# Transposing probabilities on VectorE and through DRAM instead of on TensorE, with scores three units ahead

## The chip, the cores and the metric

The kernel runs on one core of a Trainium2 chip. The core has five engines that run their own instruction streams and meet only at semaphores: TensorE (PE) for matrix products, VectorE (DVE), ScalarE (ACT), GpSimd (POOL), and SyncE (SP), which in this kernel issues every DMA. [...] DMAs move data between DRAM and SBUF. The metric is device time in microseconds of one execution.

## The reference

The input is x, eight blocks (batches) of 128 tokens with 512 features, and a context of the same shape. Four layers follow each other, each added to x after a layernorm: a one-head cross attention, a linear layer with a routed low-rank part, a cross attention with 32 query heads on 8 key/value heads, and a feed-forward layer whose weights are integers.

```python
x = x + xattn0(layernorm(x), ctx, ...)
x = x + W @ layernorm(x) + b + routed low-rank part
x = x + xattn1(layernorm(x), ctx, mask, ...)
x = x + ffn1(layernorm(x), ...)
# xattn1, for each of 32 heads of 128 features, 4 query heads to a key/value head:
q, k = rmsnorm(q) * q_norm_w, rmsnorm(k) * k_norm_w
attn = softmax(q @ k.T / sqrt(128) + mask)        # 128 queries, 128 keys
out  = concat_heads(attn @ v) @ o_proj_w.T
# ffn1: W[g, i] = (int_w - zero[group of 128, i]) * scale[group of 128, i]
y = (silu(h @ gate) * (h @ up)) @ down            # 512 -> 1792 -> 512
```

In the third layer there are eight blocks and eight key/value heads, so 64 pairs of a block and a head. One such pair, with its four query heads, is a *unit*. Every unit projects queries (512 x 512), scores (four 128 x 128 products), takes a softmax, multiplies by the values and projects the outcome (512 x 512) into x.

## The kernel before

[...] Scores are plain fp32 matmuls. A cut is a copy to the rounding format on ACT and a subtraction on DVE (split_fast, lines 64 to 66), or both on POOL (split_pool, lines 60 to 62).

The time has three stages. Up to about 210 us the first two layers run, and the keys and values of all heads are made and written to DRAM (kv_part, kv_out). The attention follows in 64 rounds up to about 710 us. The last stage is the feed-forward layer, in 14 chunks of 128 of the 1792 hidden features. In the first and the last stage a planner orders most of the instructions; in the attention (`tc.manual_schedule()`, line 790) and at the end of the last stage (line 980) every engine runs its instructions in the order in which the program is written, so an instruction that waits holds up all that stand behind it on its engine.

A round is written out in the list ROUND (line 738). Its entries are pairs of an offset and a step: in round n the step works on unit n + offset. The steps of a unit, with the engine of each:

- q_mm (PE): 12 matmuls of the query projection into PSUM. q_ssq (ACT): the sums of squares. q_rms (POOL): the norm factors (lines 346 and 348). q_turn (DVE): the queries times the factors (line 517), then a transpose of each 32x32 square (line 523) into qb. q_write (SP): qb to DRAM. q_read (SP): four DMAs of 64 KB back into qT, arranged so that features lie on partitions and each column holds a query.
- s_mm (PE): four scores products, 8 instructions (line 543). s_max (DVE): adds the mask and takes the maximum. s_exp (ACT): four exponentials with their sums. s_norm: reciprocal on DVE (line 563), scaling on POOL (line 565).
- p_mm (PE): four transposes of the probabilities by a product with the identity into PSUM (line 570). p_cut: the cut of the outcome, ACT (line 574) and DVE (line 575). av_mm (PE): three matmuls with the values. av_cut: the cut, ACT (line 591) and DVE (line 592). o_mm (PE): 12 matmuls of the output projection. o_add (DVE): adds into x (line 604).

The entries in quotation marks are places for background work by round: "load" (weights of coming heads, keys and values from DRAM), "cut" (their cut on POOL), "int" and "sub". The last two prepare the feed-forward weights: int_dma loads a tile of integers and, spread over the partitions by the DMA, its zero points; int_sub subtracts on DVE (line 631) and writes the outcome to DRAM (wint). This is done for 42 tiles, one a round.

Scores run one unit ahead of the output projection, and the query projection four units ahead. The tail has its own list TAIL. While the last rounds run, the feed-forward layer begins: for the first NE = 3 chunks, the gate and up products of the first 512 tokens run as fillers (early_unit, FILL, BANKS), as the layernorm of those tokens (norm_x, norm_turn) is done by then. For these chunks the last stage makes only the second 512 tokens. In the last stage each chunk has four gate units, four up units and four down units (up_unit, down_unit), evicted by ACT (line 875 or 878) or DVE (line 881), sums on POOL (lines 879 and 906), silu on ACT, the product on DVE (line 917), and a cut on ACT (line 921) and POOL (line 928).

Of the kernel before, what the change touches and what calls it, by code (L numbers as in the profile page):

```python
# [34 lines left out]
def f32(ap):  # L35
    return ap.bitcast(F32)
# [3 lines left out]
def tile_layers(ctx: ExitStack, tc: tile.TileContext, t, out: bass.AP):  # L40
# [76 lines left out]
    NE = 3  # L117
# [328 lines left out]
    mask_sb = wk.tile([P, NQ, P], F32, name="mask_sb", bufs=1)  # L446
    ps_q = pool(l1s, "ps_q", 2, PSUM)
# [12 lines left out]
    qps, qss, rqs, qbs, q_d, qTs, sps, nms, sms, prs, tps, pTs, avs, aTs, pos = ({} for _ in range(15))  # L460
# [20 lines left out]
    def k_load(g, hf):  # L481

        kTt[g, hf] = pk.tile([P, NQ, HB, SQ], F32, name="kT")
        for k in range(NQ):
            nc.sync.dma_start(
                kTt[g, hf][k * SQ : (k + 1) * SQ].rearrange("p i b a -> p i (b a)"),
                kT_d[g, hf][:, k, :].rearrange("(i c) e -> c i e", c=SQ),
            )

    def v_load(g, hf):  # L490
        for i, (d, p) in enumerate(((vht, "h"), (vlt, "l"))):
            d[g, hf] = pv.tile([P, HB, HD], F32R, name=f"v{p}")
            nc.sync.dma_start(f32(d[g, hf]).rearrange("p b d -> p (b d)"), v_d[g, hf][i])
# [10 lines left out]
    def q_ssq(u):  # L504
        ssq = qss[u] = small.tile([P, NREP], F32, name="qssq")
        for r in range(NREP):
            junk = wk.tile([P, HD], F32, name="junkq", bufs=2)
# [7 lines left out]
    def q_turn(u):  # L515
# [6 lines left out]
        qb = qbs[u] = wk.tile([P, NQ, NREP, SQ], F32, name="qb")  # L522
# [3 lines left out]

    def q_write(u):
        q_d[u] = dram.tile([P, NQ, NREP * SQ], F32, name=f"q_d{u}")
        nc.sync.dma_start(q_d[u], qbs.pop(u).rearrange("p j r a -> p j (r a)"))

    def q_read(u):

        qTs[u] = wk.tile([P, NQ, NREP * SQ], F32, name="qT", bufs=8)
        for j in range(NQ):
            nc.sync.dma_start(
                qTs[u][j * SQ : (j + 1) * SQ], q_d[u][:, j, :].rearrange("(i c) e -> c i e", c=SQ)
            )
# [29 lines left out]
    def p_mm(u):  # L567
        tp = tps[u] = ps_tr.tile([P, NQ, P], F32, name="tr")
        for r in range(NQ):
            nc.tensor.transpose(tp[:, r, :], prs[u][:, r, :], ident)  # L570

    def p_cut(u):
        ph, pl = pTs[u] = tuple(pat.tile([P, NQ, P], F32R, name=f"pT_{p}") for p in "hl")
        nc.scalar.copy(ph, tps[u])  # L574
        nc.vector.tensor_tensor(pl, tps[u], f32(ph), ALU.subtract)  # L575
# [10 lines left out]
    def av_cut(u):  # L586
        ah, al = aTs[u] = tuple(pat.tile([P, NREP, P], F32R, name=f"aT_{p}") for p in "hl")

        src = avs[u].rearrange("p i (r a) -> p r i a", a=SQ)
        hp, lp = (x.rearrange("p r (i a) -> p r i a", a=SQ) for x in (ah, al))  # L590
        nc.scalar.copy(hp, src)  # L591
        nc.vector.tensor_tensor(lp, src, f32(hp), ALU.subtract)  # L592
# [18 lines left out]
    def int_dma(m, c):  # L611
        wi, zi = (
            wk.tile([P, NREP, P], F32, name="qT", bufs=8).bitcast(I32).rearrange("p r c -> p (r c)")
            for _ in range(2)
        )
        staged[m, c] = (wi, zi)
        if m == "down":
            nc.sync.dma_start(wi, t["down_w"][c * P : (c + 1) * P, :])
            nc.sync.dma_start(zi, t["down_z"][c : c + 1, :].to_broadcast([P, D]))
        else:  # L620
            cols = slice(c * P, (c + 1) * P)
            nc.sync.dma_start(
                wi.rearrange("p (g c) -> p g c", c=P), t[m + "_w"][:, cols].rearrange("(g p) c -> p g c", p=P)
            )
            nc.sync.dma_start(
                zi.rearrange("p (g c) -> p g c", c=P), t[m + "_z"][:, cols].unsqueeze(0).to_broadcast([P, KT, P])
            )

    def int_sub(m, c):
        wi, zi = staged.pop((m, c))  # L630
# [441 lines left out]
```

## Time and profile before

| | |
|---|---|
| time, median of 3 runs | 883.45 us (882.79 to 884.38) |
| the profiled execution's own time | 884.13 us |
| its span in the profile | 882.3 us |
| PE busy | 852.1 us (97%) |
| DVE busy | 626.7 us (71%) |
| POOL busy | 517.5 us (59%) |
| ACT busy | 438.7 us (50%) |
| bytes moved by DMA | 141.07 MB, mean 160 GB/s |
| transposes of the probabilities (line 570) | 256 instructions, 40.1 us busy |
| query writes and reads | 64 of 256 KB and 256 of 64 KB |

The busy time of an engine counts the durations of its instructions. On PE they overlap: a matmul's duration runs from its start to the last result, while the next one has long begun, so starts tell more than durations. A group's line shows the line of the program, engine, operation, the tile written and those read, shapes and count, then busy time and mean duration, and behind the bar the idle time of the engine just before these instructions and what ended it. PEclk is the clock that was granted to TensorE, in tenths of full speed. PEld are the weight loads, which run beside the matmuls.

### The profile page before, as it was taken

To read this page: it belongs to the slowest core of one execution; us is meant where nothing else is said; L and a number is where in the kernel's file an instruction comes from. 1 tells how busy PE (TensorE), PEld (TensorE's weight loads), DVE (VectorE), ACT (ScalarE), POOL (GpSimd) and SP (SyncE) were. 2 spreads that over 40 slices of the span, in tenths; PEclk is the share of its full clock that TensorE was granted. 3 is DMA by queue.
4 is the path that set the end of the run, shared out by engine and by line. 5 is a ranking of instruction groups with operands and counts; after the bars stand their busy time and mean duration, and the time that the engine had idled before them with its cause. 6 is when DMAs were issued, how large, how long until landed. Compare 5 with 4: busy or idle time off the path is not lost.

```text
span 882.3 us, 14414 instructions
## 1 busy us (share of the span) xinstructions
PE 852.1 (97%) x4568; PEld 716.2 (81%) x4568; DVE 626.7 (71%) x1049; ACT 438.7 (50%) x1565; POOL 517.5 (59%) x571
## 2 busy tenths in 40 slices
PE   6999999999999999999999999999999989999976
PEld 5889999899787888888888888888778767788764
DVE  6613797775766677777777677666786887888877
ACT  5324444243544454455544444445555668666652
POOL 4551684234565455555555555775554568899884
PEclk9999999999999999999999999999999999999999
DMA  8522441435787788878788886644344412222103
GB/s 295 138 96 97 143 145 72 134 105 168 237 253 227 221 245 240 218 242 243 229 237 239 243 238 210 187 145 138 110 129 144 132 34 73 72 72 72 48 13 109
DMA packets 141182, 141.07 MB, mean 160 GB/s; under 512 B 17969, under 2 KB 92465, under 8 KB 141105
## 3 DMA queue, kind: packets, MB, share of 16 engines
q1 hardware_dynamic: 141104, 140.14, 53.3%
q8 instruction: 37, 0.61, 0.3%
q14 instruction: 41, 0.33, 0.1%
HBM read 97.62 MB, written 42.47 MB: 159 GB/s over the span
## 4 chain that ended last, share of the span: by engine, by line
PE 79%; DVE 6%; POOL 5%; DMA 5%; issue 2%; ACT 2%; SPq 1%; DVEq 0%; ACTq 0%; POOLq 0%
PE mm L74 8%; PE mm L76 8%; PE mm L75 8%; PE f L870 6%; PE f L871 6%; PE o L76 6%; PE s L543 6%; PE o L75 6%; PE o L74 6%; PE tr L570 3%; PE kv L76 3%; PE kv L75 3%; PE kv L74 3%; DMA qT<-q_d 2%; PE o L584 1%
## 5 line engine op out<-in xcount | busy, mean ns | idle before, releaser
L565 POOL TENSOR_TENSOR pr<-pr,rs 128x512 f32<-128x512 f32 x64 | 66.6, 1040 | 179.6 <-DVE rs L563 176.7
L604 DVE TENSOR_TENSOR xs<-o,xs 128x512 f32<-128x512 f32 x64 | 44.2, 691 | 95.5 <-PE o L76 95.5
L74 PE MATMUL mm<-wq_l,xnT_h 128*128 128x512 f32 x256 | 105.4, 412 | 0.0
L76 PE MATMUL o<-wo_h,aT_l 128*128 128x512 f32 x256 | 100.0, 391 | 0.7 <-DVE aT_l L592 0.7
L74 PE MATMUL o<-wo_l,aT_h 128*128 128x512 f32 x256 | 100.1, 391 | 0.2 <-DVE wo_l L66 0.2
L76 PE MATMUL mm<-wq_h,xnT_l 128*128 128x512 f32 x256 | 100.2, 391 | 0.0
L75 PE MATMUL mm<-wq_h,xnT_h 128*128 128x512 f32 x256 | 100.0, 391 | 0.0
L75 PE MATMUL o<-wo_h,aT_h 128*128 128x512 f32 x256 | 99.7, 390 | 0.0
L574 ACT CAST pT_h<-tr 128x512 fp32r<-128x512 f32 x64 | 37.5, 585 | 121.2 <-PE tr L570 121.2
L557 ACT ACTIVATE pr<-s,nm 128x128 f32<-128x128 f32 x256 | 90.8, 373 | 3.2 <-DVE nm L551 3.0
L591 ACT CAST aT_h<-o 128x512 fp32r<-128x512 f32 x64 | 37.6, 587 | 106.9 <-PE o L584 106.9
L74 PE MATMUL kv<-wkv_l,cT_h 128*128 128x256 f32 x256 | 73.6, 288 | 0.0
L508 ACT ACTIVATE junkq<-mm 128x128 f32<-128x128 f32 x256 | 67.3, 279 | 12.4 <-PE mm L76 6.1
L76 PE MATMUL kv<-wkv_h,cT_l 128*128 128x256 f32 x256 | 73.3, 286 | 0.0
L75 PE MATMUL kv<-wkv_h,cT_h 128*128 128x256 f32 x256 | 72.9, 285 | 0.0
L543 PE MATMUL s<-kT,qT 128*128 128x128 f32 x512 | 68.0, 276 | 1.9 <-DMA qT<-q_d 1.9
L348 POOL TENSOR_TENSOR rrq<-msq,nhalf 128x4 f32<-128x4 f32 x64 | 64.7, 1011 | 5.3
L543 PEld LDWEIGHTS s<-kT,qT 128*128 128x128 f32 x512 | 62.3, 192 | 3.0 <-DMA qT<-q_d 2.8
L575 DVE TENSOR_TENSOR pT_l<-tr,pT_h 128x512 fp32r<-128x512 f32 x64 | 44.0, 688 | 22.8 <-ACT pT_h L574 22.8
L76 PEld LDWEIGHTS o<-wo_h,aT_l 128*128 128x128 f32 x256 | 48.1, 188 | 11.6 <-DVE aT_l L592 1.5
L76 PEld LDWEIGHTS mm<-wq_h,xnT_l 128*128 128x128 f32 x256 | 48.1, 188 | 10.7
L74 PEld LDWEIGHTS o<-wo_l,aT_h 128*128 128x128 f32 x256 | 48.1, 188 | 10.7 <-DVE wo_l L66 0.6
(234 smaller groups left out, 2445.0 us busy)
## 6 DMA issues: line engine op xcount, KB each, us to landing
q_d<-qb SPq DMA_DIRECT2D x64, 256.0 KB, 2.4
qT<-q_d SPq DMA_DIRECT2D x256, 64.0 KB, 3.1
wst<-in_qpT SPq DMA_DIRECT2D x36, 256.0 KB, 3.5
wst<-in_opT SPq DMA_DIRECT2D x36, 256.0 KB, 3.1
wkv<-in_kvT SPq DMA_DIRECT2D x8, 512.0 KB, 4.3
v_d<-vh SPq DMA_DIRECT2D x16, 256.0 KB, 2.1
v_d<-vl SPq DMA_DIRECT2D x16, 256.0 KB, 2.3
kT_d<-kT SPq DMA_DIRECT2D x16, 256.0 KB, 2.6
```

The costliest lines, as they stand in the source:

```text
L74: nc.tensor.matmul(o, ah, bl, start=start, stop=False)
L75: nc.tensor.matmul(o, ah, bh, start=False, stop=False)
L76: nc.tensor.matmul(o, al, bh, start=False, stop=stop)
L348: nc.gpsimd.tensor_tensor(r[:, :n], ms[:, :n], nhalf[:, :n], ALU.pow)
L508: nc.scalar.activation(junk, qps[u][:, r * HD : (r + 1) * HD], AF.Square, accum_out=ssq[:, r : r + 1])
L543: nc.tensor.matmul(sp[:, r, :], qTs[u][:, r, :], kTt[blocks[j]][:, :, i, :], start=True, stop=True)
L557: nc.scalar.activation(pr[:, r, :], sps[u][:, r, :], AF.Exp, bias=nms[u][:, r : r + 1], accum_out=sm[:, r : r + 1])
L565: nc.gpsimd.tensor_tensor(pr, pr, rs.unsqueeze(2).to_broadcast([P, NQ, P]), ALU.mult)
L575: nc.vector.tensor_tensor(pl, tps[u], f32(ph), ALU.subtract)
L604: nc.vector.tensor_tensor(x, pos[u], x, ALU.add)
L870: nc.tensor.matmul(ps[:, hf, :], w, rl, start=True, stop=False)
L871: nc.tensor.matmul(ps[:, hf, :], w, rh, start=False, stop=True)
```

## The change

In the attention:

- p_mm is gone. In its place p_turn transposes each 32x32 square of the probabilities on DVE, p_write writes the outcome to DRAM in one DMA and p_read reads it back in one DMA, so that keys lie on partitions. The cut of the outcome (p_cut) now reads SBUF, and its subtraction runs on POOL.
- q_read is one DMA in place of four. Both reads put the rows on partitions in another order (feature c of square j on partition 4c + j instead of 32j + c), so keys and values are loaded in that order too; the key load is one DMA in place of four.
- Scores run three units ahead of the output projection, the query projection six. The rounds begin at -6, and the last key/value blocks, which stood ahead of the rounds, are put into rounds -6 to -2 ("kv"). TAIL is gone.
- Zero points are loaded once, four DMAs for all tiles (zc). int_sub spreads them over the partitions by a transpose on DVE. Integer weights come from the host in tiles of whole rows; the work is done in three of four rounds.
- Fewer buffers: qT 6 in place of 8, qb and junkq 1 in place of 2.

Around it: five early chunks in place of three, with their fillers behind s_max of the last six rounds; the second layernorm's transposes use another PSUM pool; near the end of the last stage the cast of the product is a step of its own (cast) and stands behind the next silu.

```diff
-    NE = 3
+    NE = 5
...
+        nc.sync.dma_start(
+            kTt[g, hf].rearrange("p i b a -> p i (b a)"), kT_d[g, hf].rearrange("(i c) j e -> (c j) i e", c=SQ)
+        )
...
+    def write(src, name):
+        d = dram.tile([P, NQ, NREP * SQ], F32, name=name)
+        nc.sync.dma_start(d, src.rearrange("p j i a -> p j (i a)"))
+        return d
+
+    def read(dst, d):
+
+        nc.sync.dma_start(dst, d.rearrange("(i c) j e -> (c j) i e", c=SQ))
+
     def q_write(u):
-        q_d[u] = dram.tile([P, NQ, NREP * SQ], F32, name=f"q_d{u}")
-        nc.sync.dma_start(q_d[u], qbs.pop(u).rearrange("p j r a -> p j (r a)"))
+        q_d[u] = write(qbs.pop(u), f"q_d{u}")
 
     def q_read(u):
 
-        qTs[u] = wk.tile([P, NQ, NREP * SQ], F32, name="qT", bufs=8)
-        for j in range(NQ):
-            nc.sync.dma_start(
-                qTs[u][j * SQ : (j + 1) * SQ], q_d[u][:, j, :].rearrange("(i c) e -> c i e", c=SQ)
-            )
+        qTs[u] = wk.tile([P, NQ, NREP * SQ], F32, name="qT", bufs=6)
+        read(qTs[u], q_d[u])
...
-    def p_mm(u):
-        tp = tps[u] = ps_tr.tile([P, NQ, P], F32, name="tr")
-        for r in range(NQ):
-            nc.tensor.transpose(tp[:, r, :], prs[u][:, r, :], ident)
+    def p_turn(u):
+        pb = pbs[u] = wk.tile([P, NQ, NQ, SQ], F32, name="pb", bufs=1)
+        nc.vector.transpose(
+            pb.rearrange("p j i a -> p i j a"), prs.pop(u).rearrange("p i (j c) -> p i j c", c=SQ)
+        )
+
+    def p_write(u):
+        p_d[u] = write(pbs.pop(u), f"p_d{u}")
+
+    def p_read(u):
+
+        tps[u] = wk.tile([P, NREP, P], F32, name="pT")
+        read(tps[u], p_d[u])
 
     def p_cut(u):
-        ph, pl = pTs[u] = tuple(pat.tile([P, NQ, P], F32R, name=f"pT_{p}") for p in "hl")
+        ph, pl = pTs[u] = tuple(pat.tile([P, NREP, P], F32R, name=f"pT_{p}") for p in "hl")
         nc.scalar.copy(ph, tps[u])
-        nc.vector.tensor_tensor(pl, tps[u], f32(ph), ALU.subtract)
+        nc.gpsimd.tensor_tensor(pl, tps[u], f32(ph), ALU.subtract)
...
     def int_sub(m, c):
-        wi, zi = staged.pop((m, c))
-        nc.vector.tensor_tensor(wi.bitcast(F32R), wi, zi, ALU.subtract)
+
+        z = wk.tile([P, NREP, HD], F32, name="q", bufs=1).rearrange("p r d -> p (r d)")
+        nc.vector.transpose(
+            z.rearrange("p (b a) -> p b a", a=SQ),
+            zc[:, MS.index(m), c, :].unsqueeze(2).to_broadcast([P, D // SQ, SQ]),
+        )
+        wi = staged.pop((m, c))
+        nc.vector.tensor_tensor(wi.bitcast(F32R), wi, z, ALU.subtract)
         nc.sync.dma_start(wint[m, c], wi.bitcast(F32))
...
-    FILL = {(NU - 1, p_cut): 3, (NU - 1, s_norm): 2}
-    for n in range(NU - 4, NU - 1):
-        FILL[n, p_cut], FILL[n, s_norm] = 1, 3 if n == NU - 2 else 2
+    FILL = {}
+    for n, m in zip(range(NU - 6, NU), (4, 4, 5, 5, 5, 3)):
+        FILL[n, s_max] = m
...
     ROUND = [
-        (1, s_mm), (3, q_rms), (0, p_cut), (4, q_mm, (0,)), (1, s_max), (0, av_mm), "int", (2, q_read),
-        (0, av_cut), (3, q_turn), (4, q_mm, (1, 2, 3)), (1, s_exp), "load", (3, q_write), "cut", "sub",
-        (0, o_mm), (1, s_norm), (4, q_ssq), (1, p_mm), (0, o_add),
+        "kv", (4, q_read), (5, q_rms), (3, s_mm), (6, q_mm, range(KT)), "cut", (2, p_read), (3, s_max), "int",
+        (3, s_exp), (5, q_turn), (5, q_write), "load", (3, s_norm), (1, av_mm), "sub", (3, p_turn),
+        (3, p_write), (1, av_cut), (6, q_ssq), (2, p_cut), (0, o_mm), (0, o_add),
     ]
...
-        for n in range(NU):
+        kv(-6, NG - 2, 0, 0, 2)
+        at(-6, "load", kv_cut, NG - 1)
+        kv(-5, NG - 2, 1, 0, 2)
+        kv(-4, NG - 1, 0, 0, 2)
+        kv(-3, NG - 1, 1, 0)
+        kv(-2, NG - 1, 1, 2)
+        for n in range(-6, NU):
...
             round_(n)
         norm_turn(NB - 2)
         fillers(3)
         norm_x(NB - 1)
-        fillers(len(fill) - 2)
+        fillers(len(fill) - 4)
         norm_turn(NB - 1)
         fillers(len(fill))
...
         gated(ORDER[-2])
-        rest(ORDER[-2])
         downs("A")
         up_unit("up", 0, c)
         silu(c)
+        cast(ORDER[-2])
+        rest(ORDER[-2])
```

## The prediction

> **What bounds the kernel now.** I read the busy times and the slices first, then the groups of instructions, then one round of the attention on TensorE (PE) as a timeline, then the chain that ended last, and last the waits at the end of the kernel. Busy times and slices of the page:
>
> ```profile
> PE 852.1 (97%) x4568; PEld 716.2 (81%) x4568; DVE 626.7 (71%) x1049; ACT 438.7 (50%) x1565; POOL 517.5 (59%) x571
> ```
>
> ```profile
> PEclk9999999999999999999999999999999999999999
> DMA  8522441435787788878788886644344412222103
> ```
>
> PE is never out of work, at full clock; the others have 29% to 50% to spare; the DMA engines are at 7 to 8 tenths while the attention rounds run. From the groups (busy, mean ns | idle before, and its releaser):
>
> ```profile
> L570 PE MATMUL tr<-ident,pr 128*128 128x128 f32 x256 | 40.1, 279 | 0.7 <-POOL pr L565 0.6
> L604 DVE TENSOR_TENSOR xs<-o,xs 128x512 f32<-128x512 f32 x64 | 44.2, 691 | 95.5 <-PE o L76 95.5
> L565 POOL TENSOR_TENSOR pr<-pr,rs 128x512 f32<-128x512 f32 x64 | 66.6, 1040 | 179.6 <-DVE rs L563 176.7
> ```
>
> VectorE (DVE) spends 95.5 us waiting for PE, GpSimd (POOL) 176.7 us for a row sum; PE waits 0.7 us for its transposes. A busy time is no price on PE, because matmuls overlap; the price is the step from one start to the next. PE in one round (start, duration):
>
> ```profile
> 404.19 0.39 PE L76 MATMUL o<-wo_h,aT_l 128*128 128x512 f32 x1
> 404.42 0.65 PE L570 MATMUL tr<-ident,pr 128*128 128x128 f32 x4
> 404.91 1.06 PE L543 MATMUL s<-kT,qT 128*128 128x128 f32 x8
> 405.72 0.47 PE L74 MATMUL mm<-wq_l,xnT_h 128*128 128x512 f32 x1
> 406.03 0.39 PE L75 MATMUL mm<-wq_h,xnT_h 128*128 128x512 f32 x1
> ```
>
> A 128x512 matmul steps 0.227 us, the four transposes 0.49 (404.91 - 404.42), the scores 0.81, the matmul behind them 0.31. A round of 27 large matmuls is 27 x 0.227 + 0.08 + 0.49 + 0.81 = 7.5 us, and the scores indeed start every 7.5 us from 300 us on. So a round is PE's issue time and nothing else. The chain agrees:
>
> ```profile
> PE 79%; DVE 6%; POOL 5%; DMA 5%; issue 2%; ACT 2%; SPq 1%; DVEq 0%; ACTq 0%; POOLq 0%
> ```
>
> Where PE does wait, from its timeline and the last stage's:
>
> ```profile
> 713.12 0.63 PE L97 MATMUL mm<-ident,xn 128*128 128x128 f32 x4 [1.19 <-DVE xn L91]
> 715.97 0.50 PE L870 MATMUL f<-xnT_l,wf_gate 128*128 128x512 f32 x1 [1.29 <-DVE xnT_l L99]
> ```
>
> ```profile
> 851.68 5.65 POOL L879 TENSOR_TENSOR acc<-acc,tmp 128x1024 f32<-128x1024 f32 x2
> 851.77 3.37 DVE L917 TENSOR_TENSOR th<-th,up 128x1024 f32<-128x1024 f32 x1 [0.43 <-POOL up L906]
> 855.17 1.05 ACT L921 CAST h_h<-th 128x1024 fp32r<-128x1024 f32 x1 [4.64 <-DVE th L917]
> 856.12 1.11 ACT L878 ACTIVATE tmp<-f,sd_sb 128x1024 f32<-128x1024 f32 x1
> 857.28 0.80 PE L870 MATMUL f<-xnT_l,wf_up 128*128 128x512 f32 x1 [4.48 <-ACT tmp L878]
> ```
>
> Two waits for the last layernorm; and one of 4.48 us, where an eviction on ScalarE (ACT) stands behind a cast that waits for a slow product.
>
> **The change, part by part.** The sum runs against the profiled execution: 884.13 us, span 882.3, 1.8 around it. It lies 0.7 above the median of 883.45, taken off at the end. A round is about to be 7.5 - 0.47 = 7.03 us on PE; other work must fit into that.
>
> *Transposes of the probabilities off PE.* 64 x 0.49 = 31.4 us at most. Four layernorm transposes step 0.35 (707.89 to 708.24), and a switch of format might pass to the scores behind them: at least 64 x 0.35 = 22.4. The row of the thing itself is nearer: 0.47, **-30**.
>
> [...]
>
> *What VectorE gets.* Out: the cut of the probabilities (688 ns). In: their turn, p_turn, one stream transpose (713). In 42 rounds, three of four, int_sub turns the zero points first (713) and subtracts (649). Work of a round: 0.69 mask, 0.69 maximum, 0.68 + 0.71 query, 0.16 reciprocal, 0.71, 0.69 aT_l, 0.69 xs = 5.0 us; 6.4 with int_sub. It has to wait for the four exponentials: they run 1.5 us beside 1.4 us of query work (at 407.85 to 409.35 in that round), some 0.35 with the handover. 6.75 < 7.03, so it is hidden by 0.3 us. Without that cover it costs what is over, 42 times.
>
> The subtraction reads two SBUF operands while POOL now scales the probabilities. The trace shows what that can do: the product at 851.77 took 3.37 us with POOL busy, 1.23 at 840.93 with POOL idle. The 42 subtractions of before took 647 to 651 ns each, so none was held up. Bounds: 0 to 0.4 us, the rest of a 1.04 us scaling that began at the reciprocal when the 0.71 us turn ahead is done. At 0.4 a round is 7.15.
>
> [...]
>
> *POOL* gains the cut of the probabilities, now from SBUF, at 1.29 (row of wq_l): 0.19 + 1.01 + 0.62 + 1.29 + 1.04 + 1.29 = 5.44 us. *ACT* keeps 3.8. Both fit.
>
> *The way through DRAM.* p_write and p_read join SP's queue, which loses three of four query reads (0.43 us issue each), three of four key loads and all zero-point loads, so issuing shrinks. But p_read(n+2) waits for a write of the round before; behind it stand the integer load, q_write, the weight loads and p_write, and on POOL the probability cut, the next query's norm factor, the weight cut, the scaling. That closes a loop over two rounds: turn 0.71, write W, read R, cast 0.59, cut 1.29, factor 1.2, weight cut 1.91, scaling 1.04, some 0.3 of handovers = 7.05 + W + R, plus 0.65 for a subtraction ahead of the turn. It must be under 2 x 7.03 = 14.06: W + R under 6.35. Nearest rows, issue to landing at 300 to 500 us:
>
> ```profile
> qT<-q_d SPq DMA_DIRECT2D x107, 64.0 KB, 3.7
> q_d<-qb SPq DMA_DIRECT2D x26, 256.0 KB, 2.6
> ...
> qT<-in_gate_w SPq DMA_DIRECT2D x8, 256.0 KB, 4.3
> ```
>
> W is 2.0 (the same write at 600 to 690 us, little traffic) to 2.6; R is 2.6 (a 256 KB read in the last stage) to 4.3 (256 KB in pieces of 512 B, as p_read). I take 2.5 + 3.5: p_read finds only q_read ahead of it, since SP has just stood still for the write. Loop 13.7, 6.85 a round: hidden by 0.18. At 4.6 it is hidden by far; at 6.9 a round is 7.3. For both near misses together I put in 0.06 x 56 rounds, **+3.5**. Traffic: 1.77 MB a round now (47.28 MB in 200 us); less 0.39 for zero points and the slower integers, plus 0.52, is 1.90 in 7.03 us = 270 GB/s, against slices up to 303 there. Not a bound.
>
> *Order.* Round -1 has only scores, query and one product of the values on PE (4.25 us) beside 6 us on VectorE: **+2** (-1, since key and value blocks now fill the rounds before, to 4). Waits for late query reads at 259 to 291 us (0.44 + 0.79 + 0.65) go with the zero-point loads: **-2** (0 to 2). What is late next is the cut of wo in rounds -1 and 0.
>
> *Five early chunks.* Sixteen half units of two matmuls (7.25 us) leave the last stage and go into the rounds from 58: zero on PE. There a round is 5.7 to 6.5 us of PE, less than the loop's 6.85; and rounds 54 to 57, 8.3 us long now with 2.1 us of layernorm more on VectorE, can hardly shrink: **+3.5** (0 to 7). The two layernorm waits get seven and four units as cover: **-2.5** (0 to -2.8).
>
> *Cast after the gate.* The eviction no longer stands behind it. Late next is the eviction of up's second unit on VectorE, behind the 3.37 product, until about 855.9, where PE asks at 853.6: 2.3 left of 4.48. **-2.5** (0 to -4.5).
>
> *With one answer, nothing.* The zero-point table (four loads and one copy on VectorE) and the plain integer rows lie beside key and value work, where VectorE is busy 14.8 us of 20 at 180 to 200 us. Fewer buffers (qT 6, qb and junkq 1) wait only for work a round old; if not, the wait shows as above.
>
> Sum: -30 + 3.5 + 2 - 2 + 3.5 - 2.5 - 2.5 = -28; 884.13 - 28 - 0.7 = **855 us**.
>
> **The rivals.** *The loop through DRAM takes PE's place* (ends slower). For it: one write and one read in a row, at DMA engines 82.5% busy at 300 to 500 us; zero-point loads landed after 5.1 us. Against: these loads go, and 600 to 690 us shows 2.0. At W + R = 8 the loop is 15.7, rounds are 7.85 in 42 and 7.5 in 14: 0.82 x 42 + 0.47 x 14 = 41 over 7.03, so 892. It decides from +31.5 on over rounds of 7.03 us: 0.56 a round, W + R about 7.6. A mild form (W + R 6.6 to 7.4) gives 862 to 882.
>
> [...]
>
> *The transfers are hidden wholly and the ends cost nothing*: without +3.5, +2, +3.5 it is 846.
>
> **How the numbers follow.** Near 855 (846 to 862) 0.66; VectorE 0.11; the mild loop 0.08; the loop outright 0.10; 846 or less 0.03; no change 0.02. The range 846 to 876 leaves out the 0.10, the 0.03, the 0.02 and some of the mild loop. Under 0.2% (1.8 us) this kernel's runs can't tell a change. Faster 0.88, same 0.02, slower 0.10.
>
> **What would show it.** Right: scores start every 7.0 to 7.1 us, xs (L604's successor) still waits for PE, POOL no longer waits 2.9 us per reciprocal (96.6 us in 33 at 300 to 550 us). Wrong: PE waits for pT or for aT_l; the cast of pT waits for DMA; p_read's landing over 4.3 us; the subtraction longer than 0.65 us. The prediction falls if W + R passes 7.6 us, or if PE waits in rounds -1 to 3 for more than 4 us.

## The result and the profile after

The changed kernel takes 925.67 us (median of 4 runs, 924.69 to 926.91) against 883.12 for the kernel before on the same chip (881.77 to 884.38): a ratio of 1.0486, 95% interval 1.0473 to 1.0500. The forecast was 855. The profiled execution took 924.86 us, its span is 923.1. Busy times and the chain that ended last, from the page of the changed kernel:

```profile
PE 846.8 (92%) x4312; PEld 694.9 (75%) x4312; DVE 682.8 (74%) x1104; ACT 459.4 (50%) x1581; POOL 605.3 (66%) x639
...
PE 34%; DMA 19%; POOL 18%; DVE 13%; issue 8%; ACT 5%; SPq 1%; DVEq 0%; ACTq 0%; POOLq 0%
DMA p_d<-pb 7%; PE f L859 6%; PE f L860 6%; DMA pT<-p_d 5%; DMA qT<-q_d 3%; PE mm L74 3%; PE mm L75 3%; POOL pT_l L593 3%; PE mm L76 3%; ACT pr L566 3%; POOL rrq L348 2%; DVE pb L578 2%; PE kv L76 2%; PE kv L75 2%; PE kv L74 2%
```

PE has fallen from 79% of the chain to 34%. The largest piece by line is now a transfer, the write of the probabilities (7%), and the read behind it has 5%. No engine took over as the bound; a loop through several of them did. The groups of the changed kernel's page say who waits (busy, mean ns | idle before, and its releaser):

```profile
L593 POOL TENSOR_TENSOR pT_l<-pT,pT_h 128x512 fp32r<-128x512 f32 x64 | 85.1, 1329 | 88.6 <-ACT pT_h L592 85.3
L552 PE MATMUL s<-kT,qT 128*128 128x128 f32 x512 | 73.6, 288 | 32.9 <-DMA qT<-q_d 32.5
L592 ACT CAST pT_h<-pT 128x512 fp32r<-128x512 f32 x64 | 39.6, 619 | 87.2 <-DMA pT<-p_d 83.3
```

The cast of the transposed probabilities waits 83 us for its read, and the cut on POOL behind it waits as long. The scores wait 32.5 us for the queries' read. VectorE, which used to wait 95.5 us for PE before its addition into x, waits 0.3 there.

The periods from scores to scores show no steady state. They are 7.10 or 7.11 us where nothing disturbs them, and up to 10.8 in between; rounds 0 to 53 average 8.00 us (432.2 in all, 7.60 before). In the tile names below, _h is the high part of a factor (a copy in the rounding format fp32r) and _l the rest that the copy leaves; a product is three matmuls (mm3, lines 73 to 76). PE in a disturbed and in an undisturbed round, from its timeline in the changed kernel:

```profile
412.24 0.39 PE L76 MATMUL o<-wo_h,aT_l 128*128 128x512 f32 x1
415.68 2.07 PE L552 MATMUL s<-kT,qT 128*128 128x128 f32 x8 [3.05 <-DMA qT<-q_d]
417.41 0.77 PE L74 MATMUL mm<-wq_l,xnT_h 128*128 128x512 f32 x1
...
425.74 1.06 PE L552 MATMUL s<-kT,qT 128*128 128x128 f32 x8
...
432.85 1.06 PE L552 MATMUL s<-kT,qT 128*128 128x128 f32 x8
```

The round from 425.74 to 432.85 took 7.11 us, close to the 7.03 of the forecast. The one before it lost 3 us to a late read of queries, and then, after scores of 2.07 us, ran matmuls at steps of 0.43 us in place of 0.23, because the granted clock had fallen (0.51 at 415 to 418 us, 0.52 at 418 to 422; more on this at the end).

What SyncE (SP), which issues the transfers, does in such a stretch, from its timeline in the changed kernel (start, duration):

```profile
417.96 0.37 SPq L538 DMA_DIRECT2D qT<-q_d  x1
421.88 0.37 SPq L538 DMA_DIRECT2D pT<-p_d  x1
422.34 0.46 SPq L533 DMA_DIRECT2D q_d<-qb  x1
422.85 0.42 SPq L474 DMA_DIRECT2D wst<-in_qpT  x1
423.37 0.53 SPq L495 DMA_DIRECT2D vh<-v_d  x1
423.94 0.63 SPq L495 DMA_DIRECT2D vl<-v_d  x1
424.67 0.54 SPq L639 DMA_DIRECT2D wint_down<-qT  x1
426.02 0.33 SPq L533 DMA_DIRECT2D p_d<-pb  x1
426.44 0.46 SPq L538 DMA_DIRECT2D qT<-q_d  x1
431.09 0.37 SPq L538 DMA_DIRECT2D pT<-p_d  x1
```

Here is the mechanism in ten lines. SP stands still until the write of the probabilities has landed (417.96 to 421.88, 426.44 to 431.09). Once free, it issues what has piled up behind the wait: five transfers of 256 KB in 2.3 us. The next write of the probabilities, at 426.02, is issued behind these and needs 5.0 us to land, so SP stands still again and the next pile gathers. What SP waits for in 300 to 550 us, from its waits in the changed kernel (total us, times, longest):

```profile
SPq L538 <- DMA p_d<-pb: 88.2, 32, 5.6
SPq L538 <- DMA q_d<-qb: 21.0, 14, 3.0
```

The transfers of 300 to 500 us, from the changed kernel's issues (count, size, median us from issue to landing):

```profile
p_d<-pb SPq DMA_DIRECT2D x26, 256.0 KB, 4.5
qT<-q_d SPq DMA_DIRECT2D x26, 256.0 KB, 4.2
pT<-p_d SPq DMA_DIRECT2D x25, 256.0 KB, 2.9
q_d<-qb SPq DMA_DIRECT2D x25, 256.0 KB, 3.2
```

So the write took 4.5 us where the forecast had 2.5; the read took 2.9 where it had 3.5. Together 7.4, against the 6.35 that would still have been hidden.

**Where the 69 us went.** The forecast for the profiled execution was 884.13 - 28 = 856.1; it took 924.86. The table divides the span at starts on PE: the scores of rounds 0, 54 and 58, and the first matmul of the last stage. The forecast column puts the prediction's terms where they belong: 0.41 is 0.47 less the 0.06 for near misses, and of the 3.5 for the last rounds 2 keep rounds 54 to 57 at their old length and 1.5 stand in the tail. Two more units (scores and query projection, 12 x 0.227 + 0.89 = 3.6 us each) are done before round 0 and are missing at the end, and 7.25 us of fillers change sides:

| stretch | before | forecast | changed | missed by |
|---|---|---|---|---|
| start to round 0 | 220.7 | 220.7 + 7.2 + 2 = 229.9 | 234.4 | 4.5 |
| rounds 0 to 53 | 410.4 | 410.4 - 54 x 0.41 - 2 = 386.3 | 432.2 | 45.9 |
| rounds 54 to 57 (layernorm) | 33.3 | 33.3 | 39.7 | 6.4 |
| round 58 to last stage | 51.6 | 51.6 - 2.8 + 1.5 - 2.5 + 7.25 - 7.2 = 47.8 | 54.0 | 6.2 |
| last stage | 166.3 | 166.3 - 7.25 - 2.5 = 156.6 | 162.7 | 6.1 |

Two thirds of the miss lie in the plain attention rounds, the rest at the edges. The experiments took these two apart.

### The profile page after: what moved, and what is told of

Same layout as the page of the kernel before. It is cut to its first block, busy times and chain, and to the rows that moved or that the text cites. A ratio compares the mean times of both kernels' runs of the same rounds, so it can differ in the third digit from the quotient of the medians.

```text
span 923.1 us, 14034 instructions
## 1 busy us (share of the span) xinstructions
PE 846.8 (92%) x4312; PEld 694.9 (75%) x4312; DVE 682.8 (74%) x1104; ACT 459.4 (50%) x1581; POOL 605.3 (66%) x639
## 3 DMA queue, kind: packets, MB, share of 16 engines
q1 hardware_dynamic: 153488, 164.06, 55.5%
## 4 chain that ended last, share of the span: by engine, by line
PE 34%; DMA 19%; POOL 18%; DVE 13%; issue 8%; ACT 5%; SPq 1%; DVEq 0%; ACTq 0%; POOLq 0%
DMA p_d<-pb 7%; PE f L859 6%; PE f L860 6%; DMA pT<-p_d 5%; DMA qT<-q_d 3%; PE mm L74 3%; PE mm L75 3%; POOL pT_l L593 3%; PE mm L76 3%; ACT pr L566 3%; POOL rrq L348 2%; DVE pb L578 2%; PE kv L76 2%; PE kv L75 2%; PE kv L74 2%
## 5 line engine op out<-in xcount | busy, mean ns | idle before, releaser
L593 POOL TENSOR_TENSOR pT_l<-pT,pT_h 128x512 fp32r<-128x512 f32 x64 | 85.1, 1329 | 88.6 <-ACT pT_h L592 85.3
L552 PEld LDWEIGHTS s<-kT,qT 128*128 128x128 f32 x512 | 66.5, 197 | 49.5 <-DMA qT<-q_d 28.4
L552 PE MATMUL s<-kT,qT 128*128 128x128 f32 x512 | 73.6, 288 | 32.9 <-DMA qT<-q_d 32.5
L574 POOL TENSOR_TENSOR pr<-pr,rs 128x512 f32<-128x512 f32 x64 | 68.8, 1076 | 47.5 <-DVE rs L572 47.5
L578 DVE STREAM_TRANSPOSE pb<-pr 128x512 f32<-128x512 f32 x64 | 45.2, 706 | 54.9 <-POOL pr L574 52.4
L592 ACT CAST pT_h<-pT 128x512 fp32r<-128x512 f32 x64 | 39.6, 619 | 87.2 <-DMA pT<-p_d 83.3
L521 DVE TENSOR_TENSOR q<-mm,rrq 128x512 f32<-128x512 f32 x64 | 44.0, 687 | 47.2 <-POOL rrq L348 46.5
L512 ACT ACTIVATE junkq<-mm 128x128 f32<-128x128 f32 x256 | 72.7, 284 | 9.6 <-PE mm L76 3.4
L74 PEld LDWEIGHTS mm<-wq_l,xnT_h 128*128 128x128 f32 x256 | 49.5, 193 | 13.2 <-issue 3.7
L346 POOL TENSOR_SCALAR msk<-kssq 128x2 f32<-128x2 f32 x32 | 7.1, 221 | 77.2 <-ACT junk L397 76.3
L76 PEld LDWEIGHTS mm<-wq_h,xnT_l 128*128 128x128 f32 x256 | 48.8, 191 | 11.4
```

What stands on the lines that cost most here:

```text
L74: nc.tensor.matmul(o, ah, bl, start=start, stop=False)
L76: nc.tensor.matmul(o, al, bh, start=False, stop=stop)
L512: nc.scalar.activation(junk, qps[u][:, r * HD : (r + 1) * HD], AF.Square, accum_out=ssq[:, r : r + 1])
L552: nc.tensor.matmul(sp[:, r, :], qTs[u][:, r, :], kTt[blocks[j]][:, :, i, :], start=True, stop=True)
L574: nc.gpsimd.tensor_tensor(pr, pr, rs.unsqueeze(2).to_broadcast([P, NQ, P]), ALU.mult)
L578: nc.vector.transpose(pb.rearrange("p j i a -> p i j a"), prs.pop(u).rearrange("p i (j c) -> p i j c", c=SQ))
```

## The experiments

Every ratio is to the kernel before, run beside it (medians of 882.66, 882.84 and 883.03 us in the three groups of runs). Theory D is that the way of the probabilities through DRAM and SP's queue closes a loop longer than PE's round. Theory V is that VectorE has become too full. Theory P, added after the first four, is that POOL has two weight cuts to make in some rounds.

**Transposes back on PE, all else as changed**

```diff
+    def p_mm(u):
+        tp = tps[u] = ps_tr.tile([P, NQ, P], F32, name="tr")
+        for r in range(NQ):
+            nc.tensor.transpose(tp[:, r, :], prs[u][:, r, :], ident)
...
-        nc.gpsimd.tensor_tensor(pl, tps[u], f32(ph), ALU.subtract)
+        nc.vector.tensor_tensor(pl, tps[u], f32(ph), ALU.subtract)
...
-        "kv", (4, q_read), (5, q_rms), (3, s_mm), (6, q_mm, range(KT)), "cut", (2, p_read), (3, s_max), "int",
-        (3, s_exp), (5, q_turn), (5, q_write), "load", (3, s_norm), (1, av_mm), "sub", (3, p_turn),
-        (3, p_write), (1, av_cut), (6, q_ssq), (2, p_cut), (0, o_mm), (0, o_add),
+        "kv", (4, q_read), (5, q_rms), (3, s_mm), (6, q_mm, range(KT)), "cut", (2, p_mm), (3, s_max), "int",
+        (3, s_exp), (5, q_turn), (5, q_write), "load", (3, s_norm), (1, av_mm), "sub",
+        (1, av_cut), (6, q_ssq), (2, p_cut), (0, o_mm), (0, o_add),
```

The values are then loaded in their natural order of rows.

> The changed kernel with one part undone: the probabilities are transposed on TensorE again (p_mm, four transposes a unit into PSUM, the cut's subtraction back on VectorE, values loaded in natural row order); all else stays. Theory D (the way of the probabilities through DRAM, a write of 4.5 us and a read of 2.9 us in SP's in-order queue, closes a loop over two rounds of about 15 us and sets the round): rounds fall to 7.5 us, the wait of ScalarE for pT on DMA is gone, 875 to 890 us. [...]

Measured: 897.21 us, 1.0168 [1.0132, 1.0203]. The rounds are flat, 7.54 and 7.57 in turn; the stretch from round 0 to 53 took 408.0 us (before 410.4). VectorE still has the turn of the zero points. So in the plain rounds the way of the probabilities is the whole loss, and VectorE's zero points cost nothing there. This kernel takes the cut of the probabilities off POOL as well, so it doesn't part the way through DRAM from POOL's load; the runs below do. The second finding was not expected: although its rounds are as quick as those of before, the kernel is 14 us slower. That lies at the edges: start to round 0 234.9 (220.7 + 7.2 = 227.9 would be even), rounds 54 to 57 36.8 (33.3), last stage 163.2 (166.3 - 7.25 = 159.1 would be even).

**The loads behind the probabilities' write on SP**

```diff
-        (3, s_exp), (5, q_turn), (5, q_write), "load", (3, s_norm), (1, av_mm), "sub", (3, p_turn),
-        (3, p_write), (1, av_cut), (6, q_ssq), (2, p_cut), (0, o_mm), (0, o_add),
+        (3, s_exp), (5, q_turn), (5, q_write), (3, s_norm), (1, av_mm), "sub", (3, p_turn),
+        (3, p_write), "load", (1, av_cut), (6, q_ssq), (2, p_cut), (0, o_mm), (0, o_add),
```

> The changed kernel with the background loads (weights, keys, values, early weights) moved behind p_write on SP's queue; VectorE's, ScalarE's, GpSimd's and TensorE's orders stay. Theory D, with the write late because two to four loads of 256 KB issued in the 2 us before it stand ahead of it in the DMA rings: its landing falls from 4.5 to about 3.2 us, the loop by 1.3, rounds by 0.6 us, 885 to 895 us. Theory V: nothing on VectorE or GpSimd moves, 920 to 926 us. If the write is slow for another reason than what stands ahead of it, its landing stays at 4.5.

Measured: 917.21 us, 1.0392 [1.0356, 1.0428]. Faster than the change by 8 us, not by the 30 to 40 that D gave. Landing times of this kernel at 300 to 600 us say why (last column):

```profile
pT<-p_d SPq DMA_DIRECT2D x39, 256.0 KB, 4.4
...
p_d<-pb SPq DMA_DIRECT2D x38, 256.0 KB, 2.1
```

The write now lands in 2.1 us, but the read has the loads ahead of it and needs 4.4 in place of 2.9. The sum fell only from 7.4 to 6.5. About half of the rounds are 7.1 to 7.2 us, and once in eight one of 9 to 11 follows. There SP issued a weight load and both halves of a block's values right ahead of the two reads (484.50 to 487.25 in SP's timeline), and the read of the queries took 5.86 us. From the chain of waits in that window:

```profile
486.61 5.86 DMA qT<-q_d
...
492.60 1.13 PE s L552 x8
```

The loads can be put ahead of the write or of the read; either way something queues behind them that a later round waits for.

**The integer work behind it, too**

```diff
-        (3, s_exp), (5, q_turn), (5, q_write), "load", (3, s_norm), (1, av_mm), "sub", (3, p_turn),
-        (3, p_write), (1, av_cut), (6, q_ssq), (2, p_cut), (0, o_mm), (0, o_add),
+        (3, s_exp), (5, q_turn), (5, q_write), (3, s_norm), (1, av_mm), (3, p_turn),
+        (3, p_write), "load", "sub", (1, av_cut), (6, q_ssq), (2, p_cut), (0, o_mm), (0, o_add),
```

> As the run before, and int_sub with its write also moved behind the turn of the probabilities and p_write. Theory D: landing of the write about 2.5 us, and 0.65 to 1.4 us of VectorE work no longer ahead of the turn: loop under 14 us, rounds near TensorE's 7.1 us, 860 to 875 us. Theory V: the same work on VectorE in another order, still 915 to 925 us.

Measured: 943.56 us, 1.0688 [1.0653, 1.0723]: the slowest of all, where D had expected a gain. The write lands in 2.0 us and SP hardly waits for it any more, but a new wait is there. The waits of this kernel at 300 to 650 us (total us, times, longest):

```profile
ACT pr L566 <- DVE nm L560: 144.2, 35, 6.3
DVE pb L578 <- POOL pr L574: 62.7, 42, 3.5
```

The turn stands on VectorE and waits for POOL's scaling. In the run before, which differs only in the place of the integer work, these two waits were 55.5 and 31.3 us over the same stretch. With the integers ahead of it VectorE had 1.4 us of other work while POOL scaled; now it stands idle, the maximum of the next scores comes late, and the exponentials behind that. The subtraction that the forecast took for a cost in the loop (0.65) was in part a cover in it.

**Scores four units ahead: the loop gets a third round** (e4_four_ahead)

```diff
-        "kv", (4, q_read), (5, q_rms), (3, s_mm), (6, q_mm, range(KT)), "cut", (2, p_read), (3, s_max), "int",
-        (3, s_exp), (5, q_turn), (5, q_write), "load", (3, s_norm), (1, av_mm), "sub", (3, p_turn),
-        (3, p_write), (1, av_cut), (6, q_ssq), (2, p_cut), (0, o_mm), (0, o_add),
+        "kv", (5, q_read), (6, q_rms), (4, s_mm), (7, q_mm, range(KT)), "cut", (2, p_read), (4, s_max), "int",
+        (4, s_exp), (6, q_turn), (6, q_write), "load", (4, s_norm), (1, av_mm), "sub", (4, p_turn),
+        (4, p_write), (1, av_cut), (7, q_ssq), (2, p_cut), (0, o_mm), (0, o_add),
```

(with the loads and cuts of the query weights, the key loads and the first rounds one round earlier)

> The changed kernel with scores four units ahead and the query projection seven (p_read stays two ahead, so it comes two rounds after its write, and the loop runs over three rounds). Work of every engine and all transfers stay. Theory D: 15.1 us over three rounds is 5 a round, SP no longer waits for the write, rounds at TensorE's 7.05 to 7.2 us, 855 to 870 us. Theory V: no change, 915 to 925 us.

Measured: 901.62 us, 1.0224 [1.0191, 1.0258]. 24 us better than the change. SP no longer waits for the write at all (no such line among its waits). The loads still stand ahead of the write in the program's order, but fewer of them go out in a burst just before it. Landing times of this kernel at 300 to 500 us:

```profile
pT<-p_d SPq DMA_DIRECT2D x27, 256.0 KB, 3.7
...
p_d<-pb SPq DMA_DIRECT2D x26, 256.0 KB, 2.8
```

The write takes 2.8 us in place of 4.5, with the same transfers in less time. Its landing goes with the number of transfers that SP has issued in the 4 us before it. In the two kernels together, over the 65 writes at 300 to 550 us, it is 2.1 us with one or two of them, 2.8 with three, 4.0 with four and 5.0 with five or six (medians). The changed kernel has 4.5 on average, this one 3.1. So the burst made the write slow, and not the traffic as a whole. Still, some three rounds in eight are longer than 7.5 us, most of these 8.0 to 8.6. POOL in such a stretch, from its timeline:

```profile
421.80 0.62 POOL L61 TENSOR_SCALAR wo_h<-wst 128x512 fp32r<-128x512 f32 x1
422.50 1.30 POOL L62 TENSOR_TENSOR wo_l<-wst,wo_h 128x512 fp32r<-128x512 f32 x1
423.76 0.62 POOL L61 TENSOR_SCALAR wq_h<-wst 128x512 fp32r<-128x512 f32 x1
424.47 1.29 POOL L62 TENSOR_TENSOR wq_l<-wst,wq_h 128x512 fp32r<-128x512 f32 x1
425.71 1.49 POOL L574 TENSOR_TENSOR pr<-pr,rs 128x512 f32<-128x512 f32 x1
427.17 1.28 POOL L593 TENSOR_TENSOR pT_l<-pT,pT_h 128x512 fp32r<-128x512 f32 x1
```

Two weight cuts in a row, 3.8 us, and POOL is never idle. With the new cut of the probabilities such a round costs POOL 0.19 + 1.01 + 3.83 + 1.49 + 1.28 and gaps, 8.1 us, and the scaling stands behind the cuts. This is theory P. The double cuts are the change's own work. In the kernel before the cuts of wq fell on rounds 0 to 3 of each eight and those of wo on 4 to 7, one a round (the first set of weights and rounds 44 to 47 aside). The change projects the queries two units earlier and so cuts wq two rounds earlier, which puts two of its four cuts into rounds that cut wo as well. The description of the change does not name this:

```diff
-            n = u0 - 10 + k if v > 1 else k // 2
...
-            at(n + 2, "cut", load_cut, "q", v, k)
...
+                at(u0 - 10 + k, "cut", load_cut, "q", v, k)
```

Four units ahead they are another round earlier, so that three rounds in eight have two cuts.

**One weight cut per round**, first on the change, then on the version four ahead (there 3 in place of 2):

```diff
             if v:
-                at(u0 - 6 + k, "load", load_dma, "o", v, k)
-                at(u0 - 4 + k, "cut", load_cut, "o", v, k)
+                o0 = u0 - (0 if u0 == wsets[v - 1][1] + HB else 2)
+                at(o0 - 6 + k, "load", load_dma, "o", v, k)
+                at(o0 - 4 + k, "cut", load_cut, "o", v, k)
```

> The changed kernel with the cuts of wo (and their loads) two rounds earlier, except for the set that follows after four units. In the changed kernel the cuts of wq fall on rounds 6, 7, 0, 1 of each eight and those of wo on 4, 5, 6, 7, so that GpSimd has two cuts (3.8 us) in two rounds of eight and none in two others; here there is one in each round. Theory P (GpSimd's double cuts put rounds over TensorE's 7.1 us: 1.2 + 3.8 + 1.04 + 1.29 = 7.35 us of work, on the loop): 12 to 14 rounds get 1.9 us shorter on the loop of two rounds, some 12 us: 910 to 916 us. Theory D (the loop through DRAM alone): the longer loop rounds are spread, 920 to 926 us.

> Scores four units ahead (as e4_four_ahead) and the cuts of wo three rounds earlier, so that again each round has one cut, where the run before had two in three rounds of eight. Theory P: the long rounds of e4_four_ahead (8.0 to 8.5 us, three of eight) go to about 7.2, 24 x 0.9 = 20 us: 878 to 886 us. If those rounds have another cause (VectorE's in-order waits): 895 to 902 us.

Measured: 917.58 us, 1.0401 [1.0361, 1.0441], and 886.23 us, 1.0043 [1.0027, 1.0059]. The first lies between the two ranges, 1.6 us above P's and 2.4 below D's, and its runs spread from 913.8 to 922.5, so by itself it decides little. The second is just above the range that P gave for it and 9 us below the other. With one cut but three ahead, SP still waits 92.5 us for the write; four ahead with one cut, the rounds are 7.10 and 7.11 without a break for most of 300 to 550 us. This gives the price of each cause, in a square of four kernels:

| | two cuts in some rounds | one cut per round |
|---|---|---|
| three units ahead | 925.7 | 917.6 |
| four units ahead | 901.6 | 886.2 |

The loop costs 24 to 31 us, the double cuts 8 to 15, both together 39; the step of 8, in the upper row, is uncertain by some 4 us. Here the second repair was worth more once the first was made.

**No turn of the zero points**, with the mask subtracted in their place:

```diff
-        z = wk.tile([P, NREP, HD], F32, name="q", bufs=1).rearrange("p r d -> p (r d)")
-        nc.vector.transpose(
-            z.rearrange("p (b a) -> p b a", a=SQ),
-            zc[:, MS.index(m), c, :].unsqueeze(2).to_broadcast([P, D // SQ, SQ]),
-        )
+        z = mask_sb.rearrange("p i c -> p (i c)")
```

> The changed kernel without the turn of the zero points: int_sub subtracts a constant tile (the mask's) instead, so that the zero points are left out; the subtraction with two SBUF operands, all transfers and orders stay. Takes 0.71 us from VectorE in 42 rounds. Theory V (VectorE's work sets the rounds): 42 x 0.71 = 30 us off, about 896 us. Theory D: the turn is off the loop's path except where the scaling on GpSimd is done before it: 0 to 10 us off, 915 to 925 us.

Measured: 928.25 us, 1.0519 [1.0476, 1.0563]. Taking 42 x 0.7 us off VectorE bought nothing (2.6 us more than the change, within what its runs spread): theory V falls. SP waits for the write as long as before (84.2 us at 300 to 550).

**The layernorm's turn behind the query's** (e7_and_norm_later), on the version four ahead with one cut:

```diff
-            if it[1] is s_exp and n - 2 in norms:
+            if it[1] is q_write and n - 2 in norms:
                 norm_turn(norms[n - 2])
```

> As the run before, and the layernorm transposes of rounds 54 to 57 and 62 to 63 called after q_write instead of after s_exp, so that VectorE turns the queries before it waits for the layernorm's copy on ScalarE, which stands behind the exponentials. In the changed kernel these rounds take 9 to 11 us. If that wait (2.1 us of VectorE in each) makes them long: 6 to 9 us off the run before, 870 to 880 us. If the layernorm's own work does it: no change.

Measured: 884.17 us, 1.0018 [1.0008, 1.0029]. Only 2 us of the 6 to 16 expected: the wait for that layernorm's cast, 2.13 us a round in the change, is gone here, but it was not what fills these rounds; rounds 54 to 57 still take 8.2 to 11.7 us. PE's step in the plain rounds can be read here. Scores start every 7.11 us, and between products of the projections PE steps 0.230 (0.2273 before; both over 300 to 550 us). 27 x 0.0027 is the 0.07 that is missing to 7.03. The first kernel above, with the transposes back on PE, shows 0.230 as well, so it comes with some other part of the change; which one was not tried.

**The old end of the last stage** (e9_old_tail: cast with the product, before the silu), on that version:

```diff
         gated(ORDER[-2])
+        rest(ORDER[-2])
         downs("A")
...
         silu(c)
-        cast(ORDER[-2])
-        rest(ORDER[-2])
         up_unit("up", 1, c)
```

(and the cast back inside `gated`)

> e7_and_norm_later with the end of the last stage as in the kernel before (the cast belongs to the product again and the rest follows at once). The term of the prediction was -2.5 us for the new order; in the changed kernel the wait of 4.48 us has become one of 3.93 behind VectorE. If the new order is worth what it was put at: 886 to 888 us. If the wait only changed its name: 883 to 885 us, the same within what can be told.

Measured: 889.39 us, 1.0065 [1.0047, 1.0084], above both ranges; with integers in every round (below) the two ends differ by 0.7 us only, 882.49 against 881.75. The profiles show one wait on PE that changes its name. PE's timeline with the old end:

```profile
860.10 0.79 PE L860 MATMUL f<-xnT_l,wf_up 128*128 128x512 f32 x1 [6.80 <-ACT tmp L868]
```

And with the new end, from the version with the later layernorm turn:

```profile
858.29 0.79 PE L860 MATMUL f<-h_l,wf_down 128*128 128x512 f32 x1 [3.92 <-DVE up L871]
```

With five early chunks the old order waits 6.80 us, more than the 4.48 of the kernel before; the new order waits 3.92. So the new order is worth 1 to 5 us there (889.39 - 884.17 and 0.7), but against an old end that waits longer than it did in the kernel before. What made it longer, the five early chunks or something else, was not tried.

**Integer work in each of rounds 0 to 42**, first on the version with the later layernorm turn (e10_int_each_round); then that with the old end of the last stage (e11_both); then both with the first wo loads one round earlier:

```diff
-        at(i * 4 // 3, "int", int_dma, m, c)
-        at(i * 4 // 3 + 1, "sub", int_sub, m, c)
+        at(i, "int", int_dma, m, c)
+        at(i + 1, "sub", int_sub, m, c)
```

The third of these has besides:

```diff
-        at(k // 2 - 3, "load", load_dma, "o", 0, k)
+        at(k // 2 - 4, "load", load_dma, "o", 0, k)
```

> e7_and_norm_later with the integer work in each of the first 42 rounds, as in the kernel before, instead of in three of four up to round 56. Rounds 54 to 57, which hold the layernorm, lose 1.4 us of VectorE work each; rounds 0 to 42 have it all. If VectorE's work sets the layernorm rounds (8 to 12 us now) and not the others: 4 to 7 us off, 877 to 881 us. If VectorE is near its limit in all rounds with integer work, rounds 1 to 42 grow from 7.1 to 7.3 us and more, and nothing is won: 884 to 892 us.

> e9_old_tail and e10_int_each_round together: the sum of what the two do against e7_and_norm_later, 876 to 882 us if the integer work in each round helps.

> e11_both with the first four loads of wo one round earlier. In e7_and_norm_later TensorE loses some 12 us between 200 and 260 us, and VectorE stands 1.4 us for such a load before its cut. If that load holds up the start: 2 to 4 us less than e11_both. If the start is long because the query's way through DRAM has nothing to hide it there (waits of 1.5, 3.0 and 1.2 us for query reads): the same as e11_both.

Measured: 881.75 us, 0.9978 [0.9960, 0.9996]; 882.49 us, 0.9985 [0.9969, 1.0001]; 881.97 us, 0.9988 [0.9969, 1.0006]. The first is the best version found, and its gain over the kernel before is hardly more than what can be told from none. Rounds 0 to 53 take 390.1 us there, 4 more than the forecast. Against the version with the later layernorm turn they lost 3.0 us and rounds 54 to 57, which the run was aimed at, only 1.3. Its profiled execution took 880.05 us, some 24 over the forecast's 856.1, and most of that is at the edges: start to round 0 240.2 (with one unit more done ahead, 229.9 + 3.6 = 233.5 was forecast), rounds 54 to 57 38.2 (33.3), from there to the last stage 46.1 (47.8 - 3.6 = 44.2), last stage 163.8 (156.6). The earlier wo loads changed nothing that can be told, so the cut of wo, which the forecast named as late next, isn't what the first rounds wait for. In the version with the later layernorm turn the first waits on PE are for reads of queries:

```profile
215.59 1.16 PE L552 MATMUL s<-kT,qT 128*128 128x128 f32 x8 [1.52 <-DMA qT<-q_d]
229.06 2.01 PE L552 MATMUL s<-kT,qT 128*128 128x128 f32 x8 [2.98 <-DMA qT<-q_d]
```

Why these reads come late while key and value blocks are being written was not taken apart.

## Why the prediction was wrong, point by point

**"Transposes off PE, -30": right in kind and nearly in size.** The steady round went from 7.50 to 7.53 to 7.11 us where nothing else holds it, 0.39 to 0.42 in place of 0.47: 25 to 27 us over 64 rounds. The rest is the longer step of the matmuls, for which the forecast had no term. Where both sides have that step (transposes back on PE, 7.54 and 7.57 in turn, against 7.11 four ahead with one cut), they are worth 0.45 a round, 29 us. The step in the trace of before, 0.49 us for the four, was a good base for the estimate.

**"W taken 2.5 ... R is 3.5": this is the step that failed.** Its reason was that SP stands still for the write, so the read finds the queue empty. That was right for the read (2.9). But the standing also decides what goes ahead of the *next write*: all that waited behind SP goes out in one burst just before it, and W became 4.5. The row that the forecast took W from, the write of the queries at 2.0 to 2.6, belonged to a kernel in which SP stood 23.5 us of 300 to 550 for a write to land (the changed kernel: 88.2 for the probabilities and 21.0 for the queries). With W + R = 7.4 the loop is 7.05 + 7.4 + 0.65 = 15.1 over two rounds, 7.55 a round, where the forecast had 6.85. The version with one cut a round and three units ahead, which is left with little but the loop, averages 7.73 in rounds 0 to 39, so some 0.2 a round is not in this sum. The rival "the loop through DRAM takes PE's place" was the right one, and had 0.10; its 892 us at W + R = 8 was still too low.

**"The weight cut 1.91" in the loop: right for most rounds, wrong for two in eight.** Cuts of wq and wo meet there, 3.8 us, and the loop is 17.0 over two rounds, 8.5 a round. The forecast took one cut a round from the kernel before, where that held, and did not see that the change moves the cuts of wq onto those of wo. The rival's break-even, 7.6 us of W + R, was too lenient, since it counted neither these rounds nor the waits for queries: the kernel lost at 7.4 already, and with rounds of 8.00 on average.

**"p_read ... behind it stand ...": named, not priced.** The forecast listed what is queued behind SP's wait, and priced only the loop of the probabilities. The write of the queries is in that list. It goes out late, SP then stands 21.0 us of 300 to 550 for it before it can read the queries back, the reads land in 4.2 us, and PE waits 32.5 us for them in the whole run.

**VectorE hidden by 0.3 us: it did not become the bound (0.11), though the hold-up was larger than thought.** The 42 subtractions took 1.19 us each in the changed kernel (50.2 us in all) where 0.65 had been measured, so the hold-up by POOL is 0.54, above the upper bound of 0.4. All 42 ran beside an instruction of POOL and took 0.94 to 1.58 us; of the 42 before, at 0.65, none did. One of them beside POOL, and what POOL's cut takes at the same time, from the timeline of the changed kernel:

```profile
422.14 0.94 DVE L638 TENSOR_TENSOR qT<-qT,q 128x512 fp32r<-128x512 int32 x1
422.64 1.61 POOL L62 TENSOR_TENSOR wq_l<-wst,wq_h 128x512 fp32r<-128x512 f32 x1
```

Both are longer when they meet: 0.94 and 1.61 us here, 0.65 and 1.29 to 1.30 alone. So these two engines do not meet at semaphores only. The longer subtractions cost nothing visible while VectorE had other slack: the version four ahead with one cut runs at PE's pace with 1.28 us a subtraction. The 0.06 a round that the forecast had put in for this and for the loop together was an estimate that no run shows by itself.

**Ramp "+2" and layernorm rounds "+3.5 (0 to 7)": under-sized.** Measured against the forecast the start is 4.5 us worse, rounds 54 to 57 6.4 and the rounds to the last stage 6.2; the experiment with transposes on PE, with no way of the probabilities through DRAM, has about as much at the start (5.0) and half as much in rounds 54 to 57 (3.5). "8.3 us long now ... can hardly shrink" assumed that they would not grow. They took 8.1, 10.5, 11.4 and 9.8. In these four rounds the exponentials now wait for the maximum on VectorE, from the waits of the changed kernel at 666.6 to 706.3 us (total us, times, longest); in the same rounds before it was 0.2 us:

```profile
ACT pr L566 <- DVE nm L560: 18.5, 3, 6.4
```

With transposes on PE it is 20.8 us, and with no integer work left in these rounds 18.6 still. So the amount of VectorE's work alone does not explain it; which part of the change brings the wait was not found.

**"Five early chunks ... zero on PE; cast after the gate, -2.5": the last stage failed both.** It should have lost 7.25 us of PE and 2.5 of a wait, and it lost 3.6 in all. The wait went from 4.48 to 3.93: what the forecast named as late next, up's eviction behind the slow product, is indeed what PE waits for, but later than the 855.9 that it worked with. From the timeline of the last stage of the changed kernel:

```profile
894.68 3.35 DVE L905 TENSOR_TENSOR th<-th,up 128x1024 f32<-128x1024 f32 x1 [2.88 <-POOL up L895]
897.95 0.74 DVE L870 SCALAR_TENSOR_TENSOR up<-f,su_sb,up 128x512 f32<-128x512 f32 x1
...
898.74 0.80 PE L859 MATMUL f<-h_l,wf_down 128*128 128x512 f32 x1 [3.93 <-DVE up L870]
```

The product itself now waits 2.88 us for a sum on POOL, and only then runs its 3.35. Over the whole last stage, what PE's steps have beyond 0.227 us sums to 14.3 us before and 18.1 after, so 3.8 of the 7.25 us that left PE came back. Only 0.2 of it are longer waits (7.9 and 8.1 us); 2.0 are matmuls at half the granted clock (0.50 to 0.53) behind waits (17 of them after, 7 before). What makes the rest was not traced.

## What to carry to other kernels

A detour through DRAM is not priced by the landing time that a transfer shows today: here SP, which stood still for one transfer, sent out afterwards, in one burst, what had piled up behind it (five transfers in 2.3 us), and the next transfer of the loop paid for the burst (5.0 us to land, against the 2.0 to 2.6 that the forecast had read off). Work out such a loop with the worst round of the schedule as the change leaves it, not with a usual one, and give it a round more of distance before anything else; here a list of offsets was worth 24 to 31 us. Before work is moved from the bound engine, ask how much the move can give at its best (25 us here) against the number of paths with less than half a microsecond of room that it crosses.

## What the runs showed of the hardware

PE's granted clock fell to about half behind some waits and stayed at 1.00 behind others. In the changed kernel, from 200 us on, it was 0.50 to 0.53 behind waits of 3.23 us (scores at 227.65), 3.05 (415.68), 3.56 (586.30), 1.82 (759.55) and 3.93 (898.74), and 1.00 behind eight waits of 1.52 to 1.80 us. After the wait of 3.05 at 412.6 to 415.7 of the changed kernel (windows: PE, PEld, DVE, ACT, POOL busy, then PEclk, DMA share, GB/s):

```profile
408.00:415.00 7.00, 4.63 (x20) 3.31 (x19) 4.91 (x8) 3.36 (x17) 6.54 (x8) 1.00 0.66 203
415.00:418.00 3.00, 2.32 (x10) 2.22 (x11) 1.94 (x4) 0.62 (x1) 1.79 (x3) 0.51 0.99 311
418.00:422.00 4.00, 4.00 (x11) 3.13 (x10) 3.29 (x6) 1.51 (x8) 3.67 (x6) 0.52 0.84 278
422.00:426.00 4.00, 4.00 (x21) 3.30 (x20) 1.77 (x4) 2.47 (x10) 3.31 (x4) 1.00 0.67 199
```

This wait of 3 us so costs some 6: ten matmuls at 0.42 us or more in place of 0.23 are 2 more, and the scores took 2.07 us in place of 1.06. The length of one wait does not decide it. Two scores, the first from PE's timeline of the version with one cut a round and three ahead, the second from that with scores four ahead:

```profile
430.99 1.13 PE L552 MATMUL s<-kT,qT 128*128 128x128 f32 x8 [2.06 <-DMA qT<-q_d]
236.48 1.13 PE L552 MATMUL s<-kT,qT 128*128 128x128 f32 x8 [3.11 <-DMA qT<-q_d]
```

Behind the first, with a wait of 2.06 us, PE steps 0.43 us from 432.28 to 435.27 (mean granted clock 0.63 at 431 to 435). Behind the second, with 3.11, the granted clock is 1.00 from 236 to 242. What else counts is not shown here. In the attention of the changed kernel the low clock explains a few microseconds only: the ten slow matmuls behind the wait shown, and three and two behind two others (227.65 and 586.30).
